# Layer 0's norms of four row tiles and layer 3's last norm: the inverse root as one power operation on GpSimd in a four-layer graph attention kernel

## The chip, the core and the metric

The kernel runs on one core of one Trainium2 chip. That core has five engines with a queue of instructions each: TensorE (PE in the profile; its weight loads are listed as PEld), VectorE (DVE), ScalarE (ACT), GpSimd (POOL) and SyncE (SP), which issues most transfers. The metric is the device time of one execution in microseconds, lower being better; of several runs the median counts. One execution of each kernel is recorded by the hardware profiler, instruction by instruction.

## The reference

Four graph attention layers over 4096 nodes of 256 features and one adjacency matrix in which a node has about 17 neighbours. Each layer ends in a residual sum and a norm, and this norm is what the change touches:

```python
def _layernorm(x, axis=-1, eps=1e-5):
    m = jnp.mean(x, axis=axis, keepdims=True)
    v = jnp.var(x, axis=axis, keepdims=True)
    return (x - m) / jnp.sqrt(v + eps)

# in a layer: projection h, then scores e[i, j] = leaky_relu(s[i] + d[j], 0.2) where adj[i, j],
# attn = softmax over j, out[i] = sum over j of attn[i, j] * h[j]   (4, 4, 2 and 1 heads)
x = _layernorm(x + layer0(x, adj))
x = _layernorm(x + layer1(x, adj))
x = _layernorm(x + layer2(x, adj))
x = _layernorm(x + layer3(x, adj))   # elu around two products; the output
```

## The kernel before

The nodes are cut into 32 row tiles of 128. A row tile does not look at all 4096 nodes: for each one the kernel packs the nodes that any of its rows has for a neighbour into 13 groups of 128, with one more place for the tile's own nodes. The packing (the class `Block`, lines 365 to 457) is done once, while layer 0 runs: VectorE compares (line 435, `oh`), TensorE moves masks with what comes out (line 441), and the lists of indices are finished ten row tiles ahead of their use.

For one row tile of one layer, `RowTile` does the following. `load` fetches the packed nodes' rows, 13 gathers by index issued on GpSimd (line 636, tile `G`), and the tile's own rows by SyncE (line 633). `half`, twice, makes the weights of 7 groups: products and exponentials on VectorE (lines 680 and 684) and ScalarE (line 689), then the mask on VectorE (lines 686 and 690, tile `w`), and TensorE sums the neighbours' rows under these weights (line 698). `finish` divides by the sum of the weights, adds the residual `y`, and calls `Layer.norm`. The normalised `y` goes to memory by SyncE (line 992), and, in layers 0 to 2, into a list `ready`, from which `Projection` takes it some steps later to make the next layer's rows (its transposition on TensorE is line 538). In layers 2 and 3 the last row tiles are also done without packing, four at a time (`whole_rows`, lines 929 to 940).

`norm` computes mean and variance of one row tile by two VectorE instructions (lines 969 and 970) into a table `mv`. It then waits until a group of row tiles has come together. `GROUPS` says how many: in layer 0 four for the row tiles 0 to 23 and one after that, so there are six groups of four; in layer 3 one for most, with row tile 27 (`count - 1`) the last to be finished and alone in its group. For the whole group at once, on tables of 128 by the size of the group, line 978 adds the small constant (tile `v`), and then the inverse root is computed without any root instruction: lines 980 and 981 make a first guess from the bits of the number, and three rounds of lines 985 to 988 improve it. These are fourteen VectorE instructions, each of which needs the one before. Line 990 then scales each row tile of the group.

The instructions of one engine run in the order in which they stand in its queue. This order is not quite that of the program: a scheduler plans all queues when the program is built, from its own estimates of durations, and puts ready work of later program lines between dependent instructions. Where two are ready, the one that stands earlier in the program comes first. The waits between engines are inserted by the same step. Tiles come from pools with fixed numbers of buffers; `G` of layer 0 has 16 slots, of which a row tile takes 7, so a gather may have to wait until TensorE is through with an older row tile.

Of the kernel before, what the change touches and what calls it, by code (L numbers as in the profile page):

```python
# [37 lines left out]
F32 = mybir.dt.float32  # L38
# [7 lines left out]
ALU = mybir.AluOpType  # L46
# [4 lines left out]
P = 128  # L51
# [4 lines left out]
BT = 4  # L56
# [79 lines left out]
@with_exitstack  # L136
def kernel(ctx: ExitStack, tc: tile.TileContext, ins: dict, out: bass.AP):
    nc = tc.nc
    const = ctx.enter_context(tc.tile_pool(name="const", bufs=1))
    dram = ctx.enter_context(tc.tile_pool(name="xs", bufs=1, space=DRAM))  # L140
    ident = const.tile([P, P], F32, name="ident")
    make_identity(nc, ident)
    shared = {
        "ident": ident,
        "idx": const.tile([P, NT, NP], I32, name="idx"),
        "flag": const.tile([1, 1], I32, name="flag"),
        "shift1": const.tile([P, 1], F32, name="shift1"),
        "shift2": const.tile([P, 1], F32, name="shift2"),
        "shift3": const.tile([4, 4], F32, name="shift3"),
        "zero": const.tile([4, 4], F32, name="zero"),  # L150
        "maskC": dram.tile([NT, P, NP, MC], U8, name="maskC"),
        "maskW": dram.tile([NB, P, NT, BT, MC], U8, name="maskW"),
        "d": [const.tile([P, NT, TERMS[n]], F32, name=f"d{n}") if WHOLE[n] else None for n in range(4)],
        "v": [dram.tile([N, ROW[n]], F32, name=f"vals{n}") for n in range(4)],
        "e": [dram.tile([NT, TERMS[n], P], F32, name=f"edge{n}") for n in range(4)],
        "x": [None] + [dram.tile([N, F], F32, name=f"xp{n}") for n in (1, 2, 3)],
    }
    nc.vector.memset(shared["shift1"], -KEXP)
    nc.vector.memset(shared["shift2"], -2.0 * KEXP)

    nc.vector.memset(shared["zero"], 0.0)
    nc.vector.memset(shared["shift3"], -2.0 * KEXP)
    nc.gpsimd.affine_select(out=shared["shift3"], in_=shared["shift3"], pattern=[[1, 4]], compare_op=ALU.is_gt,
                            fill=0.0, base=0, channel_multiplier=-1)
    with ExitStack() as packed:
        Program(tc, packed, ins, out, shared).run()
    general = nc.values_load(shared["flag"][0:1, 0:1], min_val=0, max_val=1,
                             skip_runtime_bounds_check_because="it is the result of a comparison")
    with tc.If(general > 0):
        dense_layers(tc, ins, out, ident)  # L170
# [553 lines left out]
class Layer:  # L724
# [237 lines left out]
    def norm(self, y, m):  # L962


        nc, ep = self.nc, self.prog.ep
        if not self.group:
            self.mv = ep.tile([P, BT, 2], F32, name="mv")
        st = ep.tile([P, 6], F32, name="st")
        nc.vector.bn_stats(st, y)
        nc.vector.bn_aggr(self.mv[:, len(self.group), :], st)  # L970
        self.group.append((y, m))
        if len(self.group) < next((size for end, size in GROUPS[self.n] if m < end), 1):
            return
        g = len(self.group)
        mv = self.mv[:, :g, :]

        v = ep.tile([P, BT], F32, name="v")[:, :g]
        nc.vector.tensor_scalar(v, mv[:, :, 1], EPS, None, op0=ALU.add)
        b = ep.tile([P, BT], I32, name="b")[:, :g]
        nc.vector.tensor_scalar(b, v.bitcast(I32), 1, None, op0=ALU.logical_shift_right)  # L980
        nc.vector.tensor_scalar(b, b, -1.0, float(0x5F3759DF), op0=ALU.mult, op1=ALU.add)
        r = b.bitcast(F32)
        u = ep.tile([P, BT], F32, name="u")[:, :g]
        for _ in range(3):
            nc.vector.tensor_tensor(u, r, r, op=ALU.mult)
            nc.vector.tensor_tensor(u, u, v, op=ALU.mult)
            nc.vector.tensor_scalar(u, u, -0.5, 1.5, op0=ALU.mult, op1=ALU.add)  # L987
            nc.vector.tensor_tensor(r, r, u, op=ALU.mult)  # L988
        for i, (y, m) in enumerate(self.group):
            nc.vector.tensor_scalar(y, y, mv[:, i, 0:1], r[:, i:i + 1], op0=ALU.subtract, op1=ALU.mult)  # L990
            dst = self.prog.out if self.n == 3 else self.shared["x"][self.n + 1]
            nc.sync.dma_start(out=dst[m * P:(m + 1) * P, :], in_=y)
            if self.n < 3:
                self.ready.append((self.step + 1, y, m))
        self.group = []
# [39 lines left out]
def dense_layers(ctx: ExitStack, tc: tile.TileContext, ins: dict, out: bass.AP, ident):  # L1035
# [361 lines left out]
    def layer(nodes, following):  # L1397
        n = nodes.n
        nxt = following() if following is not None else None
        for blk in range(NB):  # L1400
# [13 lines left out]
            else:  # L1414
# [6 lines left out]
                for it in range(BT):  # L1421
# [8 lines left out]
                    nc.vector.scalar_tensor_tensor(yt, z, 0.0, yt, op0=ALU.max, op1=ALU.add)  # L1430
                    nc.vector.scalar_tensor_tensor(yt, e, -1.0, yt, op0=ALU.add, op1=ALU.add)
            norm(y)
            dst = out if n == 3 else xD[n + 1]
            nc.sync.dma_start(out=to_tiles(dst[blk * W:(blk + 1) * W, :]), in_=y)
# [57 lines left out]
```

## Time and profile before

| | us |
|---|---|
| median of 3 runs | 2267.64 (2262.25 to 2268.71) |
| the profiled execution | 2271.01 |
| its span, first to last recorded instruction | 2269.3 |
| busy: PE, DVE, ACT, POOL | 2019.7, 1798.0, 1738.5, 1494.7 |

The span counts from the first instruction to the last; the execution's own time has 1.7 us more around it. The page of the profile cuts the span into 40 slices and gives each engine's busy share in each, in tenths. Other views give busy times by stretch, groups of instructions by line, who waited for whom, and the instructions in order of time; in the last of these, a line has the start in us from the start of the span, the duration, the engine, the line of the program, the operation, the tiles that it writes and reads, their shapes, and in brackets how long the engine was idle before it and what ended that. TensorE's busy time includes modelled ends, so a high number does not mean that it runs at its peak. From the first use of gathered rows to the last of layer 0 is about 165 to 820 us, layer 1 runs to some 1340, layer 2 to some 1750, and layer 3 to the end. The groups of instructions that belong to the fourteen are these:

```profile
L987 DVE TENSOR_SCALAR u<-u 128x1 f32<-128x1 f32 (+2 forms) x237 | 38.6, 165 | 3.6
L988 DVE TENSOR_TENSOR b<-b,u 128x1 f32<-128x1 f32 (+2 forms) x237 | 37.1, 158 | 3.7
L985 DVE TENSOR_TENSOR u<-b 128x1 f32<-128x1 f32 (+2 forms) x237 | 37.0, 158 | 3.2
L986 DVE TENSOR_TENSOR u<-u,v 128x1 f32<-128x1 f32 (+2 forms) x237 | 37.0, 158 | 3.4
L980 DVE TENSOR_SCALAR b<-v 128x1 int32<-128x1 int32 (+2 forms) x79 | 13.3, 169 | 1.0
L981 DVE TENSOR_SCALAR b<-b 128x1 int32<-128x1 int32 (+2 forms) x79 | 13.2, 169 | 1.0
```

After the count stand the group's busy time in us, the mean duration of one in ns, and the engine's idle time before them in us.

### The profile page before, as it was taken

To read this page: it belongs to the slowest core of one execution; us is meant where nothing else is said; L and a number is where in the kernel's file an instruction comes from. 1 tells how busy PE (TensorE), PEld (TensorE's weight loads), DVE (VectorE), ACT (ScalarE), POOL (GpSimd) and SP (SyncE) were. 2 spreads that over 40 slices of the span, in tenths; PEclk is the share of its full clock that TensorE was granted. 3 is DMA by queue.
4 is the path that set the end of the run, shared out by engine and by line. 5 is a ranking of instruction groups with operands and counts; after the bars stand their busy time and mean duration, and the time that the engine had idled before them with its cause. 6 is when DMAs were issued, how large, how long until landed. Compare 5 with 4: busy or idle time off the path is not lost. (4 is left out here: it accounts for less than half of the span.)

```text
span 2269.3 us, 49072 instructions
## 1 busy us (share of the span) xinstructions
PE 2019.7 (89%) x15689; PEld 1834.6 (81%) x15689; DVE 1798.0 (79%) x5317; ACT 1738.5 (77%) x4977; POOL 1494.7 (66%) x1596
## 2 busy tenths in 40 slices
PE   3878889989999959998988897989998799999996
PEld 2757878887989949998878887989997688778885
DVE  2987999999999959988888886877975465576567
ACT  4777888988889949988888877978883666676664
POOL 2107565655667777777777777777761677777773
PEclk8988999999999979999999998999998899999998
DMA  8879767877557766666666666778764788888884
GB/s 281 264 229 356 237 213 248 292 240 233 143 163 194 211 165 167 190 177 174 166 173 176 172 169 180 216 206 239 221 200 138 236 268 269 274 266 276 266 256 145
DMA packets 250318, 492.98 MB, mean 217 GB/s; under 512 B 44385, under 2 KB 156610, under 8 KB 249666
## 3 DMA queue, kind: packets, MB, share of 16 engines
q0 software_dynamic: 81536, 245.30, 38.0%
q1 hardware_dynamic: 168514, 244.46, 33.7%
q8 instruction: 126, 2.06, 0.4%
q14 instruction: 142, 1.16, 0.2%
HBM read 437.05 MB, written 52.54 MB: 216 GB/s over the span
## 5 line engine op out<-in xcount | busy, mean ns | idle before, releaser
L636 POOL DMA_INDIRECT G<-vals,idx x1456 | 1481.7, 1018 | 736.4 <-issue 188.5
L689 ACT ACTIVATE w<-S,G 128x128 f32<-128x128 f32 x3248 | 988.2, 389 | 123.0 <-DMA G<-vals,idx 109.1
L698 PE MATMUL bank<-w,G 128*65 128x128 f32 x7168 | 843.8, 277 | 97.8 <-DVE w L686 75.7
L698 PEld LDWEIGHTS bank<-w,G 128*65 128x65 f32 x7168 | 796.4, 140 | 116.5 <-DVE w L686 86.9
L701 PE MATMUL bank<-G,w 128*128 128x257 f32 (+1 forms) x2688 | 491.1, 340 | 36.1 <-DVE w L690 12.5
L701 PEld LDWEIGHTS bank<-G,w 128*128 128x128 f32 x2688 | 431.8, 193 | 86.2 <-ACT z L1004 16.6
L690 DVE SCALAR_TENSOR_TENSOR w<-w,bank 128x896 f32<-128x896 f32 x384 | 410.6, 1079 | 18.7 <-ACT w L689 18.1
L940 PE MATMUL bank<-vw,pw 128*128 128x129 f32 (+1 forms) x2048 | 299.7, 303 | 5.6 <-ACT zw L1004 2.7
L940 PEld LDWEIGHTS bank<-vw,pw 128*128 128x128 f32 x2048 | 275.7, 193 | 22.4 <-ACT zw L1004 3.1
L666 ACT ACTIVATE w<-S,G 128x128 f32<-128x128 f32 x392 | 138.0, 390 | 130.0 <-DMA G<-vals 77.6
L435 DVE TENSOR_SCALAR oh<-iota,place 128x256 bf16<-128x256 f16 (+2 forms) x992 | 225.8, 301 | 9.3 <-PE bank L441 9.3
L441 PE MATMUL bank<-mk,oh 128*128 128x132 fp8e4 x2336 | 188.6, 226 | 12.4 <-DVE oh L435 10.2
L680 DVE TENSOR_TENSOR w<-S,G 128x256 f32<-128x256 f32 x384 | 154.0, 417 | 53.0 <-DMA G<-vals,idx 49.6
L552 PE MATMUL bank<-wext,xT 128*128 128x268 f32 (+3 forms) x640 | 181.4, 417 | 15.7 <-ACT xT L543 12.8
L441 PEld LDWEIGHTS <-oh 128*128 128x128 bf16 x2336 | 148.6, 99 | 48.3 <-DVE oh L435 20.4
L380 ACT ACTIVATE mk<-raw 128x1024 uint8<-128x1024 int32 x128 | 131.1, 1054 | 25.8 <-DMA raw<-in_adjB_dram 25.1
L552 PEld LDWEIGHTS bank<-wext,xT 128*128 128x128 f32 x640 | 119.2, 203 | 35.5 <-ACT xT L543 15.7
L929 ACT ACTIVATE pw<-Sw,d 128x512 f32<-128x512 f32 x192 | 131.7, 714 | 15.6 <-PE bank L940 11.9
L937 DVE TENSOR_TENSOR pw<-pw,mw 128x512 f32<-128x512 f32 x64 | 44.1, 693 | 125.0 <-ACT pw L936 61.6
L930 DVE SCALAR_TENSOR_TENSOR pw<-pw,mw 128x512 f32<-128x512 f32 x192 | 126.7, 690 | 17.3 <-ACT pw L929 16.4
L686 DVE SCALAR_TENSOR_TENSOR w<-w,bank 128x896 f32<-128x896 f32 x128 | 138.6, 1083 | 0.8
L690 DVE SCALAR_TENSOR_TENSOR w<-w,mk 128x896 f32<-128x896 f32 x80 | 86.7, 1087 | 47.5 <-ACT w L689 44.1
(131 smaller groups left out, 1605.3 us busy)
## 6 DMA issues: line engine op xcount, KB each, us to landing
raw<-in_adjB_dram SPq DMA_DIRECT2D x128, 512.0 KB
mk<-maskC SPq DMA_DIRECT2D x112, 231.0 KB
G<-vals,idx POOLq DMA_INDIRECT x1456
S<-edge SPq DMA_DIRECT2D x64, 256.0 KB
vw<-vals SPq DMA_DIRECT2D x96, 129.0 KB
xp<-y SPq DMA_DIRECT2D x96, 128.0 KB
y<-xp SPq DMA_DIRECT2D x96, 128.0 KB
mw<-maskW SPq DMA_DIRECT2D x20, 528.0 KB
```

Of the source, the lines that this page charges most:

```text
L435: nc.vector.tensor_scalar(oh[:, :n * P], iota[:, :n * P], self.place[:, it, j:j + 1], None, op0=ALU.is_equal)
L441: nc.tensor.matmul(accs[b][:, s * MC:(s + 1) * MC], oh[:, (k - a) * P:(k - a + 1) * P], mk[:, j, it, :].bitcast(FP8), start=touches[b][0] ...
L552: nc.tensor.matmul(pp[:, :c1 - c0], self.xT[:, k, :], wext[:, k, c0:c1], start=(k == 0), stop=(k == KT - 1 and brow is None))
L636: nc.gpsimd.indirect_dma_start(out=self.place(pos), out_offset=None, in_=sh["v"][n][:NODES[t], :], in_offset=bass.IndirectOffsetOnAxis(ap= ...
L666: nc.scalar.activation(w[0][:, k, :], S[:, 0, :], AF.Relu, bias=d(k, 0))
L680: nc.vector.tensor_tensor(w[h][:, k:k + 2, :], S[:, h:h + 1, :].to_broadcast([P, 2, P]), dd[:, :, V + T + h:V + T + h + 1].to_broadcast([P ...
L686: nc.vector.scalar_tensor_tensor(w[h], w[h], LEAST, mh, op0=ALU.max, op1=ALU.mult)
L689: nc.scalar.activation(w[h][:, k, :], S[:, h, :], AF.Exp, bias=d(k, h))
L690: nc.vector.scalar_tensor_tensor(w[h], w[h], LEAST, mh, op0=ALU.max, op1=ALU.mult)
L698: nc.tensor.matmul(accs[0][:Wd, h * P:(h + 1) * P], v, w[h][:, k, :], **how)
L701: nc.tensor.matmul(a, w[h][:, k, :], v, **how)
L940: nc.tensor.matmul(accs[it][:, c:c + Wd], p[:, it, :], v[:, c:c + Wd], start=(j == 0 and h == heads[0]), stop=(j == NT - 1), skip_group_ch ...
```

## The change

For the six groups of four in layer 0 and for the last norm of layer 3, `norm` leaves the fourteen instructions out. In their place GpSimd raises `v` to the power −0.5, elementwise, in one instruction on 128 by 4 (or 128 by 1) numbers, with the exponent from a table `mhalf` that is filled once at the start. The scaling is moved into a function of its own that both ways call. All other norms are as before.

```diff
@@ -143,6 +143,7 @@
         "idx": const.tile([P, NT, NP], I32, name="idx"),
+        "mhalf": const.tile([P, BT], F32, name="mhalf"),
         "flag": const.tile([1, 1], I32, name="flag"),
@@ -155,6 +156,7 @@
+    nc.vector.memset(shared["mhalf"], -0.5)
     nc.vector.memset(shared["shift1"], -KEXP)
@@ -976,6 +978,12 @@
         nc.vector.tensor_scalar(v, mv[:, :, 1], EPS, None, op0=ALU.add)
+        if self.n == 0 and g == BT or self.n == 3 and m == self.count - 1:
+
+            r = ep.tile([P, BT], F32, name="r")[:, :g]
+            nc.gpsimd.tensor_tensor(r, v, self.shared["mhalf"][:, :g], op=ALU.pow)
+            self.scale(mv, r)
+            return
         b = ep.tile([P, BT], I32, name="b")[:, :g]
@@ -986,6 +994,10 @@
             nc.vector.tensor_tensor(r, r, u, op=ALU.mult)
+        self.scale(mv, r)
+
+    def scale(self, mv, r):
+        nc = self.nc
         for i, (y, m) in enumerate(self.group):
             nc.vector.tensor_scalar(y, y, mv[:, i, 0:1], r[:, i:i + 1], op0=ALU.subtract, op1=ALU.mult)
             dst = self.prog.out if self.n == 3 else self.shared["x"][self.n + 1]
```

## The prediction

> **What bounds the kernel now.** I read the page first, for the busy tenths of each engine, then the same by stretches of layer 0, then who waits there, then the instructions around one norm, and last the end of the program. The page shows a kernel whose bound changes:
>
> ```profile
> span 2269.3 us, 49072 instructions
> PE   3878889989999959998988897989998799999996
> DVE  2987999999999959988888886877975465576567
> POOL 2107565655667777777777777777761677777773
> ```
>
> Each digit is 57 us. From the fifth slice to the fourteenth (227 to 794 us, nearly all of layer 0) VectorE stands at 9; in the last third it falls to 4 to 7, with TensorE at 9. So the same instruction saved on VectorE is worth something in layer 0 and next to nothing later. The stretches from one norm of four to the next make it sharp (columns: length, then busy us and count of PE, PEld, DVE, ACT and POOL, the granted clock, DMA share, GB/s):
>
> ```profile
> 284.00:372.00 88.00, 78.66 (x789) 70.29 (x786) 87.60 (x273) 78.72 (x232) 52.86 (x54) 1.00 0.74 234
> 547.00:632.00 85.00, 79.91 (x789) 73.77 (x789) 84.52 (x273) 62.95 (x212) 52.72 (x53) 0.96 0.57 171
> 632.00:697.00 65.00, 62.39 (x572) 59.20 (x573) 62.53 (x157) 57.90 (x202) 45.18 (x47) 1.00 0.62 171
> 697.00:822.00 125.00, 118.72 (x1036) 113.63 (x1033) 116.89 (x357) 108.44 (x375) 95.14 (x99) 1.00 0.71 199
> ```
>
> Up to 632 us VectorE is idle 0.4 to 0.5 us in 87, and TensorE 5 to 9. The waits of TensorE from 160 to 822 us agree: 30.5 us of them end with the weights of line 686 and 9.3 us with those of line 690, both VectorE's. GpSimd has 32 us or more of each free. After 632 us, when the packing of the lists runs out, TensorE and VectorE stand within 2 us of each other.
>
> How often the changed code runs is in the answer for the line of v:
>
> ```profile
> L978 DVE TENSOR_SCALAR v<-mv x79: 140/155/310, 283.6 to 2260.1; 128x1 f32<-128x1 f32 x43, 128x2 f32<-128x2 f32 x29, 128x4 f32<-128x4 f32 x6, 128x3 f32<-128x3 f32 x1
> ```
>
> There are 79 norms; the six of width 4 are layer 0's row tiles 0 to 23, with v at 283.6, 371.1, 458.2, 546.7, 631.0 and 695.1 us. Here is VectorE in time (start, duration) around the first, then GpSimd at the same moment:
>
> ```profile
> 283.62 0.19 DVE L978 TENSOR_SCALAR v<-mv 128x4 f32<-128x4 f32 x1
> 283.72 0.27 DVE L684 TENSOR_SCALAR w<-S,G 128x128 f32<-128x128 f32 x1
> 283.92 0.16 DVE L980 TENSOR_SCALAR b<-v 128x4 int32<-128x4 int32 x1
> 283.99 0.24 DVE L435 TENSOR_SCALAR oh<-iota,place 128x128 bf16<-128x128 f16 x1
> ...
> 284.22 1.07 DVE L686 SCALAR_TENSOR_TENSOR w<-w,bank 128x896 f32<-128x896 f32 x1
> 285.22 0.15 DVE L985 TENSOR_TENSOR u<-b 128x4 f32<-128x4 f32 x1
> 285.29 1.07 DVE L690 SCALAR_TENSOR_TENSOR w<-w,bank 128x896 f32<-128x896 f32 x1
> ...
> 292.23 1.05 DVE L990 TENSOR_SCALAR y<-y,mv,b 128x256 f32<-128x256 f32 x3
> ```
>
> ```profile
> 278.18 0.95 POOL L636 DMA_INDIRECT G<-vals,idx  x1 [0.30 <-issue]
> 283.42 1.14 POOL L636 DMA_INDIRECT G<-vals,idx  x1 [4.30 <-DVE mv L970]
> 284.87 0.95 POOL L636 DMA_INDIRECT G<-vals,idx  x1 [0.31 <-DVE b L981]
> ```
>
> Two things are to be seen. The fourteen small instructions of the root are not run one after another: other work stands between them, so the order was planned, and v to y takes 8.6 us without VectorE resting. And GpSimd's gathers come in a dense row, 1.25 us from start to start, that begins just before v. Last, the end of the program, where nothing else is left:
>
> ```profile
> 2260.12 0.15 DVE L978 TENSOR_SCALAR v<-mv 128x1 f32<-128x1 f32 x1
> 2260.31 0.15 DVE L980 TENSOR_SCALAR b<-v 128x1 int32<-128x1 int32 x1
> ...
> 2262.80 0.16 DVE L988 TENSOR_TENSOR b<-b,u 128x1 f32<-128x1 f32 x1
> 2263.00 0.41 DVE L990 TENSOR_SCALAR y<-y,mv,b 128x256 f32<-128x256 f32 x1
> 2263.44 0.33 SPq L992 DMA_DIRECT2D out_dram<-y  x1
> ```
>
> **What the Trainium skill says.** "VectorE: DVE Perf Modes", section "The DRAIN you can't avoid", has it that VectorE's instructions are to be counted, not their semaphores, since the next one waits for the pipe to empty. The trace agrees in part: alone a small one costs 0.19 us (the tail), between others far less (below). "GPSIMD Engine Reference", section 3.1, gives 4497 ns for an add of 2048 elements per partition at about 2.6 cycles an element; at the page's 1.2 GHz that leaves some 60 ns of fixed cost. No page prices a power, and the trace of before has none. "Perfetto Trace Analysis", section "GPSIMD Engine Instruction", advises to take GpSimd by start-to-start spacing: here a gather shows 0.95 us and recurs every 1.25. "SBUF — State Buffer", section "Who interferes with whom", says that a GpSimd read of SBUF and a VectorE instruction with two SBUF inputs exclude each other; line 680 is one, of 0.4 us. The kernel before has no GpSimd elementwise work in layer 0, so its trace can't show this.
>
> **The change, part by part.** *Layer 0, VectorE.* Each norm of four loses 14 instructions: lines 980 and 981, and three rounds of four. In the first, the time from the start of each of the fourteen to the start of the next instruction is 0.07 us ten or eleven times, else 0.08 to 0.12, together 1.1 us. The other way: v to y holds 17 other instructions, which at their usual spacing (1.00 us for lines 686 and 690, for instance) fill 7.3 of the 8.6 us; the rest is 1.3 us. The second way gives 1.1 to 1.3 us for the five norms up to 631 us. I take 1.15: five of them, 5.8 us, on an engine with no idle time, so on the path. The sixth lies where VectorE and TensorE are level: I take half, 0.5 us. That is 6.3 us, as long as TensorE, idle 5 to 9 us a stretch there, doesn't take over at 1.15.
>
> *Layer 0, GpSimd.* One power is added per norm, with two waits: it for v, and the first scaling (line 990) for it. Crossing from VectorE to GpSimd took 0.07 us at the start of the program (the table bt: 13.54 to 13.61); I take the same back. The power on 128x4: below, the smallest dependent GpSimd operations there (0.28 us); above, 2 us, an estimate of mine at seven times that, for a function made of many steps. I take 0.8. Before it there may be a gather in progress, up to 1.25 us, and a read held off by line 680, up to 0.4. So the root lands 0.9 to 3.8 us after v, most likely about 1.5, where it took 7.3 to 8.3 until now. Behind the power stand the gathers of two tiles further on; a delay of 1 us is nothing to them (VectorE's waits for gathers in 160 to 822 us are 3.2 us in all). Behind the waiting scaling stands everything of VectorE: the masked weights that TensorE waits for. This costs nothing if the plan puts lines 684, 435 and 686 in between, as now (1.4 us at their spacing), and the lateness in full if not. I take nothing, and 0 to 2.5 us each as the bounds.
>
> *The last norm of layer 3.* From line 980 to the scaling there are 2.69 us with nothing beside. In their place: 0.07 + 0.8 + 0.07, with the usual 0.04 us of crossing already in the old spacing: some 0.9. The gain is 1.8 us on the path (bounds 2.3 and 0.5), as the output's transfer starts after it. The norm before it, in 2253.7 to 2256.4, keeps its fourteen.
>
> *The fill of the table of −0.5, the tile r, the moved scaling loop:* one VectorE instruction of some 0.06 us at the start, when the engine is idle for 10 us; nothing.
>
> Sum: 5.8 + 0.5 + 1.8 = 8.1 us. The profiled execution of before took 2271.01 us (span 2269.3), so 2262.9 of its kind; the median of the runs is 3.4 us lower, 2267.64, which gives 2259.5.
>
> **The rivals.** *A, the forecast (0.54):* as summed, own range 2255 to 2263.
>
> *B, the saving is given back (0.21):* waits of about 0.7 us for the root at each of six norms take 4 us, or TensorE and its clock (0.96 in 459 to 632 us) become the bound of these stretches. For it: TensorE is at 91 to 94% there. Against: it waits for VectorE, not the other way round. About 2264.
>
> *C, the root lands too late and VectorE stands (0.17):* the power takes 2 us or more, or is queued behind two gathers, and the scaling is put where a short power would be ready. Landing 4.5 us after v with 1.4 us of cover is a stop of 3.1 us, six times 18.6; less the 6.3 saved and with 0.5 left of the tail, 11.8 slower: 2279. It decides from a stop of 1.2 us per norm on, where 6.3 + 0.5 to 1.8 are eaten. For it: gathers are dense just after v, VectorE runs in order, and no row prices a power. Against: GpSimd is 38% free or more up to 632 us, and the power is older in the program than the gathers of tile m+3 that run there.
>
> *D, the new order helps more than its saving (0.08):* y comes 5 us earlier, and the whole plan shifts with it; TensorE's waits for line 686 in 160 to 822 us (30.5 us) shrink by a quarter: 2252.
>
> **How the numbers follow.** A measurement of this kernel tells some 0.3% from no change (6.8 us; the three runs lie within 6.5). Seven tenths of A lie below 2260.8 (0.38); with D and a tenth of B that is 0.48 for faster. The rest of A and of B, 0.16 and 0.19, is no change, 0.35. C is slower, 0.17. Range 2252 to 2274: it takes in A, B and the milder half of C.
>
> **What would show it.** 72 chains of line 988 in place of 79 (216 instructions for 237); seven powers on GpSimd, each of 0.3 to 1 us; v to y in the six norms at 1.5 to 3 us; no VectorE idle time put down to GpSimd; VectorE still without idle time to 620 us, and the sixth norm 5 to 6 us sooner; tail from v to scaling about 1.1 us instead of 2.9. Wrong it would be if the waits view has VectorE's line 990 behind GpSimd for over 1 us a time, if the sixth norm comes no sooner, or if layers 1 to 3 change length by more than 3 us, which this sum doesn't have.

## The result and the profile after

The changed kernel takes 2296.86 us (median of 4 runs, 2295.89 to 2297.24), the kernel before 2264.94 us on the same chip (4 runs, 2259.79 to 2268.71). The ratio is 1.0133, with a 95% interval of 1.0113 to 1.0154: 1.3% slower, where 8 us less were forecast. The page of the changed kernel has these lines against those of before:

```profile
span 2295.2 us, 48988 instructions
PE   4888898988988987998989898989998799999996
DVE  2887998989988977998888895878885366566566
POOL 2117655646567777777777777777871677777773
```

VectorE has 97 instructions fewer (seven times fourteen, less one fill) and is no longer solid 9 from the fifth slice on: it has less work and stands still more. The stretches from norm to norm of layer 0 say how much longer it takes (columns as before: length, busy us and count of PE, PEld, DVE, ACT, POOL, granted clock, DMA share, GB/s):

```profile
282.00:372.00 90.00, 81.88 (x791) 73.73 (x789) 86.56 (x262) 76.77 (x225) 54.36 (x55) 0.96 0.72 231
561.40:652.00 90.60, 79.72 (x786) 73.14 (x786) 82.98 (x258) 61.27 (x207) 51.52 (x54) 0.96 0.52 161
652.00:722.00 70.00, 64.68 (x574) 61.76 (x573) 62.31 (x144) 58.45 (x205) 47.07 (x48) 0.95 0.56 158
722.00:848.00 126.00, 117.28 (x1024) 114.28 (x1022) 115.11 (x339) 107.31 (x374) 96.03 (x100) 0.96 0.67 192
```

The third stretch is 70 us instead of 64, the second 90.6 instead of 84.3. From the first norm of layer 0 to its last (`v` to `v`) the changed kernel takes 561.8 us and the one before 532.3, so 29.5 us more; from there to the end of the program they take 1451.4 and 1453.4. So the loss is all in layer 0. VectorE's waits between these norms (for whom, total us, times, longest), after and then before:

```profile
DVE y L1002 <- POOL r L984: 27.3, 6, 9.6
DVE oh L437 <- PE bank L443: 9.9, 5, 2.4
DVE w L692 <- ACT w L691: 5.0, 7, 2.5
```

```profile
DVE w L690 <- ACT w L689: 1.7, 6, 0.7
DVE oh L435 <- PE bank L441: 0.2, 1, 0.2
```

There are six waits of 27.3 us in all for the power's result `r`, which the kernel before does not have, and 9.9 us for TensorE's mask products, which were 0.2 us before. Here is the second of the six in time, first VectorE, then GpSimd:

```profile
371.95 0.18 DVE L980 TENSOR_SCALAR v<-mv 128x4 f32<-128x4 f32 x1
372.04 0.24 DVE L437 TENSOR_SCALAR oh<-iota,place 128x128 bf16<-128x128 f16 x1
372.20 1.07 DVE L688 SCALAR_TENSOR_TENSOR w<-w,bank 128x896 f32<-128x896 f32 x1
377.78 1.40 DVE L1002 TENSOR_SCALAR y<-y,mv,r 128x256 f32<-128x256 f32 x4 [4.50 <-POOL r L984]
```

```profile
370.50 1.10 POOL L638 DMA_INDIRECT G<-vals,idx  x1 [3.20 <-PE bank L700]
371.91 0.98 POOL L638 DMA_INDIRECT G<-vals,idx  x1 [0.30 <-DVE mv L972]
373.20 0.96 POOL L638 DMA_INDIRECT G<-vals,idx  x1 [0.30 <-issue]
374.46 0.96 POOL L638 DMA_INDIRECT G<-vals,idx  x1 [0.30 <-issue]
375.72 0.96 POOL L638 DMA_INDIRECT G<-vals,idx  x1 [0.30 <-issue]
376.70 1.04 POOL L984 TENSOR_TENSOR r<-v,mhalf 128x4 f32<-128x4 f32 x1
```

`v` is ready at 372.13. VectorE has 1.1 us of other work left in front of the scaling and then stands for 4.5 us with its whole queue behind it. GpSimd does not take long over the power: it issues four gathers first, one every 1.26 to 1.29 us, and only then comes to the power, which takes 1.04 us. At the six norms the power starts 2.0, 4.6, 3.6, 5.0, 3.1 and 9.6 us after the end of `v` (2, 4, 3, 4, 3 and 8 gathers in front, with the one in progress), and the idle times before the scaling are 1.8, 4.5, 3.5, 4.9, 3.0 and 9.6 us.

The stops did not all cost the same. From the first of the six norms to the sixth the changed kernel takes 440.1 us for 411.5, so 28.6 us more, with 17.7 us of stops in them. From the sixth norm to the last of layer 0 it takes 121.7 us for 120.8, though the longest stop, 9.6 us, lies there. In that stretch it is GpSimd that does not rest. In the kernel before, its last longer pause in layer 0 ends at 652.74 us, and from there to the last norm 128 gathers follow each other with never more than 0.31 us between them. The place where this begins (before), and the sixth norm's power in this row (after):

```profile
645.70 0.95 POOL L636 DMA_INDIRECT G<-vals,idx  x1 [0.31 <-issue]
652.74 1.12 POOL L636 DMA_INDIRECT G<-vals,idx  x1 [6.10 <-ACT w L689]
654.17 0.95 POOL L636 DMA_INDIRECT G<-vals,idx  x1 [0.30 <-issue]
```

```profile
730.87 0.96 POOL L638 DMA_INDIRECT G<-vals,idx  x1 [0.30 <-issue]
731.85 1.04 POOL L984 TENSOR_TENSOR r<-v,mhalf 128x4 f32<-128x4 f32 x1
733.07 1.01 POOL L638 DMA_INDIRECT G<-vals,idx  x1 [0.18 <-issue]
```

The stop of VectorE does not interrupt the row: from the sixth norm to the last of layer 0 GpSimd issues 95 gathers in both kernels. So the traces speak for the row of gathers as what sets the pace there, rather than VectorE; no run tests this by itself.

At the end of the program GpSimd's queue is empty, and the forecast holds:

```profile
2284.43 0.15 DVE L980 TENSOR_SCALAR v<-mv 128x1 f32<-128x1 f32 x1
2284.74 0.57 POOL L984 TENSOR_TENSOR r<-v,mhalf 128x1 f32<-128x1 f32 x1 [18.36 <-DVE v L980]
2285.35 0.41 DVE L1002 TENSOR_SCALAR y<-y,mv,r 128x256 f32<-128x256 f32 x1 [0.76 <-POOL r L984]
```

From `v` to the scaling are 0.92 us, where it was 2.88.

### The profile page after: what moved, and what is told of

Its sections match the earlier page's. It is cut to its first block, busy times and chain, and to the rows that moved or that the text cites. A ratio compares the mean times of both kernels' runs of the same rounds, so it can differ in the third digit from the quotient of the medians.

```text
span 2295.2 us, 48988 instructions
## 1 busy us (share of the span) xinstructions
PE 2032.6 (89%) x15689; PEld 1844.6 (80%) x15689; DVE 1790.5 (78%) x5220; ACT 1739.6 (76%) x4977; POOL 1503.9 (66%) x1603
## 5 line engine op out<-in xcount | busy, mean ns | idle before, releaser
L700 PE MATMUL bank<-w,G 128*65 128x128 f32 x7168 | 853.1, 279 | 114.8 <-DVE w L688 64.8
L700 PEld LDWEIGHTS bank<-w,G 128*65 128x65 f32 x7168 | 805.3, 141 | 135.2 <-DVE w L688 74.7
L692 DVE SCALAR_TENSOR_TENSOR w<-w,bank 128x896 f32<-128x896 f32 x384 | 409.9, 1078 | 22.4 <-ACT w L691 21.5
L450 ACT ACTIVATE cm<-bank 128x396 uint8<-128x396 f32 (+1 forms) x160 | 68.7, 451 | 87.5 <-PE bank L443 86.7
```

The lines of the kernel that those rows point to most:

```text
L692: nc.vector.scalar_tensor_tensor(w[h], w[h], LEAST, mh, op0=ALU.max, op1=ALU.mult)
L700: nc.tensor.matmul(accs[0][:Wd, h * P:(h + 1) * P], v, w[h][:, k, :], **how)
```

## The experiments

Eighteen runs were made beside the kernel before, in five sets. They came to chips of two kinds, and the numbers cannot be read without this: on some the kernel before takes about 2267 us, on others 2764 to 2799 us. On the latter TensorE stands still without a releaser that the profile shows, and the clock that it was granted was 0.88 to 0.90 of full speed over a whole run, against 0.95 to 0.97 on the others; why is not known. Waits of TensorE in the whole of the kernel "late" on such a chip, and VectorE's longest in 338 to 905 us, its layer 0:

```profile
PE bank L700 <- issue: 168.1, 222, 2.5
PE bank L703 <- issue: 81.2, 73, 8.3
```

```profile
DVE oh L437 <- PE bank L443: 81.6, 72, 6.7
```

There VectorE itself has long waits for TensorE in layer 0 (81.6 us at that line, 0.2 us in the kernel before above), so these chips say little about a stop of VectorE on a chip like that of the result. The times are medians. Ratios are to the kernel before on the same chip; they come from all runs and can differ a little from the quotient of the medians. The last column is VectorE's wait for the root in the recorded execution.

| kernel | before, us | this, us | ratio (95%) | wait, us |
|---|---|---|---|---|
| the change | 2264.94 | 2296.86 | 1.0133 (1.0113 to 1.0154) | 28.1 |
| change_again | 2267.59 | 2296.80 | 1.0130 (1.0100 to 1.0161) | 29.6 |
| trip_again | 2267.59 | 2298.10 | 1.0134 (1.0104 to 1.0163) | 30.7 |
| ahead_again | 2267.59 | 2275.20 | 1.0036 (1.0023 to 1.0048) | 6.5 |
| both | 2267.59 | 2267.28 | 1.0008 (0.9994 to 1.0023) | 5.7 |
| both26 | 2268.71 | 2273.72 | 1.0020 (1.0011 to 1.0029) | 1.0 |
| both26_raw5 | 2268.71 | 2270.97 | 1.0009 (0.9996 to 1.0021) | 1.0 |
| before_raw5 | 2268.71 | 2267.84 | 0.9995 (0.9986 to 1.0004) | none |
| tail_again | 2268.71 | 2269.51 | 1.0004 (0.9992 to 1.0017) | 0.7 |
| tail | 2799.22 | 2805.04 | 1.0015 (0.9995 to 1.0036) | 0.7 |
| ahead | 2799.22 | 2803.69 | 1.0013 (0.9993 to 1.0033) | 1.8 |
| late | 2799.22 | 2792.67 | 0.9976 (0.9960 to 0.9993) | 10.3 |
| trip | 2799.22 | 2803.37 | 1.0015 (0.9999 to 1.0031) | 33.5 |
| first3 | 2766.46 | 2770.58 | 1.0018 (1.0005 to 1.0031) | 11.9 |
| five_raw5 | 2766.46 | 2764.93 | 0.9993 (0.9969 to 1.0016) | 0.8 |

The remaining four runs, all on the second kind of chip, are told below.

**The change again (change_again).** The same kernel, beside the others of its set:

> The changed kernel once more, beside the kernel before on whatever chip this is. Where the kernel before takes about 2265 us, VectorE bounds layer 0 and it should be 30 us slower, with 27 us of VectorE's waits for the root there. Where the kernel before takes about 2800 us, as in the first four experiments, TensorE stands still for 30 us of 120 without a visible reason, VectorE has idle time to give, and theory of the queue expects the same waits of 20 us or more but less than 10 us in the time. The rival, that the new order as such costs the 30 us, expects them on both.

It was 29 us slower, with the same waits at the same places. The other half of the question, the change on a chip of the second kind, was not run.

**The last norm alone (tail, tail_again).** The condition is cut to layer 3:

```diff
-        if self.n == 0 and g == BT or self.n == 3 and m == self.count - 1:
+        if self.n == 3 and m == self.count - 1:
```

> Only the last norm of layer 3 takes the power; layer 0 is as before. The trace of the change shows v to scaling there in 0.92 us where 2.88 stood, so both theories expect the time of before less 2 us, about 2263 against 2265, and layers 0 to 2 of unchanged length within 3 us. If the new order of the whole program were what costs 30 us, some of it would be seen here already: more than 5 us slower than before would speak for that.

> The power in the last norm alone, where the kernel before takes 2265: v to scaling in 0.92 us for 2.88, so 2 us less, within what can be told from no change; layer 0 as before within 3 us.

Both are no change that can be told, and in both traces `v` to the scaling takes under 1 us. In "tail_again" layer 0 keeps its length: 533.8 us from first to last norm, against 532.3 before. The 2 us are gained in the trace and are too few for the medians to show. A price of 30 us that comes with the changed program as such is excluded by "tail_again"; what a new order within layer 0 costs, this run does not say.

**The wait alone (trip, trip_again).** The fourteen instructions stay; a copy through GpSimd is put behind them in the same seven norms:

```diff
+        if self.n == 0 and g == BT or self.n == 3 and m == self.count - 1:
+            far = ep.tile([P, BT], F32, name="far")[:, :g]
+            nc.gpsimd.tensor_copy(far, r)
+            r = far
         self.scale(mv, r)
```

> The fourteen instructions are kept and a copy of the root through GpSimd is added, in the same seven norms: the wait alone, with nothing saved and no power. Theory of the queue: the copy meets the row of gathers later, 7 us after v, when it is still dense, so VectorE waits 1 to 4 us at each, 6 to 25 us in all, and the time is before plus that, 2271 to 2292. Rival (the power is slow): a copy of 0.3 us leaves waits under 0.7 us each, and the time is that of before within 5 us.

> The fourteen instructions kept, with the copy through GpSimd, which showed 33 us of waits of VectorE in the six norms of layer 0 in the first experiments. Where the kernel before takes 2265 us: the queue alone expects 25 to 45 us more, 2290 to 2310, more than the change itself, as nothing is saved; the rival of a slow power, or of a new order around a shorter chain, expects under 10 us. Where it takes 2800 us: within 8 us of before.

This is the clearest answer. The copy takes 0.20 us and there is no power in the program, yet the kernel is as slow as the change, 1.0134, and VectorE's waits, this time for the copy `far`, are of the same kind:

```profile
DVE y L1000 <- POOL far L993: 30.3, 6, 11.9
DVE rec L1026 <- PE bank L718: 3.4, 3, 1.7
```

There are 30.3 us of waits in layer 0 and 30.5 us more in the median: on this kind of chip the stops of VectorE in layer 0 cost, taken together, what they last. The sixth of them, 11.9 us, does interrupt GpSimd's row of gathers (for 5.7 us), and from the sixth norm to the last of layer 0 this kernel takes 129.7 us for 120.8. On the other kind ("trip") 33.2 us of idle time before the six scalings went with 4 us more, which is not clear of no change.

**The power ahead of the gathers (ahead, ahead_again).** The gathers of places 10 to 13 of the row tile three further on are queued behind the power of that norm:

```diff
-            nc.gpsimd.tensor_tensor(r, v, self.shared["mhalf"][:, :g], op=ALU.pow)
+            power = nc.gpsimd.tensor_tensor(r, v, self.shared["mhalf"][:, :g], op=ALU.pow)
+            if self.n == 0:
+                self.prog.power[m + 3] = power.ins
...
+            with ExitStack() as order:
+                if n == 0 and pos >= 10 and m in prog.power:
+                    order.enter_context(prog.tc.issue_after(prog.power[m]))
                 nc.gpsimd.indirect_dma_start(
```

> All seven powers stay; the gathers of places 10 to 13 of the row tile three further on are queued behind the power, which so stands ahead of them in GpSimd's queue. Theory of the queue (the power waits behind 2 to 8 gathers of 1.25 us, and VectorE's whole queue behind it): the power starts within 0.1 us of v, the root lands 1.3 us after v, VectorE's waits for GpSimd fall from 28 us to under 4, and the time is before less 3 to 8 us, 2257 to 2262. Rival (the power itself, or the crossing between engines, is slow): waits of 2 us or more each stay, and the time stays over 2285. Second rival (the new order of the other instructions): the waits go, but 9 us or more of the 32 stay.

> The power ahead of the gathers, as in the second experiment. Where the kernel before takes 2265 us: theory of the queue expects 2257 to 2263, since the fourteen instructions are gone and VectorE waits under 4 us for the root; the rival of the new order expects 2270 or more. Where it takes 2800 us: within 8 us of before.

The second norm of "ahead_again", GpSimd and then VectorE:

```profile
366.37 0.95 POOL L642 DMA_INDIRECT G<-vals,idx  x1 [0.31 <-issue]
372.04 1.04 POOL L988 TENSOR_TENSOR r<-v,mhalf 128x4 f32<-128x4 f32 x1 [4.72 <-DVE v L984]
373.28 1.14 POOL L642 DMA_INDIRECT G<-vals,idx  x1 [0.19 <-ACT w L695]
```

```profile
371.80 0.16 DVE L984 TENSOR_SCALAR v<-mv 128x4 f32<-128x4 f32 x1
372.03 1.08 DVE L692 SCALAR_TENSOR_TENSOR w<-w,bank 128x896 f32<-128x896 f32 x1
373.12 1.40 DVE L1008 TENSOR_SCALAR y<-y,mv,r 128x256 f32<-128x256 f32 x4
```

The power now starts 0.08 us after `v`, its 1.04 us lie beside line 692, and no wait is left at this norm. The ratio falls from 1.0130 to 1.0036: of 29 us of loss by medians, 22 go with the place of the power in GpSimd's queue. The first rival (a slow power or crossing) falls. But the kernel was expected at 2257 to 2263 us, faster than before, and takes 2275, where the rival of the new order was put. Of waits for the root 4.9 us remain at the sixth norm, where gathers of lower places still come first, and 0.8 at the first; VectorE's waits for ScalarE at line 696 are 7.4 us, for 1.7 at that instruction before. So the rival, that other waits take over, is alive.

**The scaling later (late, both).** The scalings of layer 0's fours are kept back half a row tile in the program: alone ("late"), and with the power ahead ("both"):

```diff
-            self.scale(mv, r)
+            if self.n == 0:
+                self.owed = (mv, r, self.group)
+                self.group = []
+            else:
+                self.scale(mv, r)
             return
...
             self.tile(m).half(part)
+        if self.owed is not None:
+            mv, r, self.group = self.owed
+            self.owed = None
+            self.scale(mv, r)
```

> All seven powers stay where they are in GpSimd's queue, and the four scalings of layer 0's groups are written half a row tile later in the program, which puts 2 to 3 more instructions of 1 us ahead of them in VectorE's queue. Theory of the queue: the power still lands 2 to 6 us after v, but 2 to 3 us more of it are covered; VectorE's waits for GpSimd fall from 28 us to 10 to 16, and the time to 2275 to 2285. Rival (new order, not the waits): no change from 2297.

> The power ahead of the gathers, and the scalings of layer 0 half a row tile later in the program: no wait for the root is left in layer 0 at all. Theory of the queue: VectorE's waits for GpSimd under 1.5 us, all in the last norm, and the time of the kernel with the power ahead less 0 to 3 us: 2255 to 2262 where before takes 2265. Rival of the new order: 2270 or more.

"late" came to a chip of the second kind: the waits fell to 10.3 us, as expected, and it was 0.24% faster there than the kernel before, the only one of all with an interval below 1; the clock granted was 0.891 in the mean of its runs and 0.889 in those of the kernel before, so this is no clean sign of the order alone. What it does on the other kind of chip was not run. "both" has no wait at the first five norms and is level with the kernel before, 1.0008: the loss is gone, but 2255 to 2262 us were expected, and the 6 us of VectorE's time and the 2 us of the tail that it saves do not show. From the first norm to the sixth it takes 413.5 us (411.5 before), from there to the last of layer 0, where the gathers run without a pause, 122.1 (120.8). Its own waits in layer 0 (282 to 819 us) tell where the time went, with ScalarE and VectorE in order of time behind them:

```profile
DVE w L696 <- ACT w L695: 7.3, 9, 2.9
DVE y L1017 <- POOL r L993: 4.9, 1, 4.9
DVE row L581 <- ACT row L579: 2.5, 2, 2.2
```

```profile
394.59 1.06 ACT L383 ACTIVATE mk<-raw 128x1024 uint8<-128x1024 int32 x1 [3.07 <-DMA raw<-in_adjB_dram]
395.55 2.72 ACT L695 ACTIVATE w<-S,G 128x128 f32<-128x128 f32 x9
```

```profile
397.72 1.09 DVE L696 SCALAR_TENSOR_TENSOR w<-w,bank 128x896 f32<-128x896 f32 x1 [2.67 <-ACT w L695]
```

In this order ScalarE converts the next adjacency rows at 387 us, where it did so at 400 us before; the fifth of them has not landed yet, ScalarE stands 3.1 us, and VectorE 2.7 us behind it. This wait did not exist in this part of the kernel before.

**The sixth norm's gathers and the rows' buffer (both26, both26_raw5, before_raw5).** "both26" is "both" with the gathers of row tile 26 held back from place 4 on; "both26_raw5" has five buffers for the adjacency rows in addition; "before_raw5" is the kernel before with the five buffers alone:

```diff
-                if n == 0 and pos >= 10 and m in prog.power:
+                if n == 0 and pos >= (4 if m == 26 else 10) and m in prog.power:
...
-        cst, rawp, mkp, ohp = pool("icst", 1), pool("raw", 4), pool("imk", 2), pool("oh", 8)
+        cst, rawp, mkp, ohp = pool("icst", 1), pool("raw", 5), pool("imk", 2), pool("oh", 8)
```

> As the kernel with the power ahead and the later scaling, but the gathers of row tile 26 are held back from place 4 on, since there the sixth power still met a gather row (a wait of 4.9 us). Theory of the queue: VectorE's waits for GpSimd under 1.5 us in all; the time 4 to 5 us below that kernel's: where before takes 2267, 2261 to 2264. If the time stays at 2267, what is left comes from elsewhere: a rival says that the granted clock or TensorE bounds layer 0 once the waits are gone.

> The same with a fifth buffer for the adjacency rows. In the kernel with the power ahead and the later scaling, ScalarE waited twice 3 us for such rows in layer 0 and VectorE behind it 5.8 us, which the kernel before does not show there. If that is where the rest of the saving went, these waits go and the time is another 3 to 6 us lower, 2256 to 2260 where before takes 2267; if TensorE bounds the stage, nothing changes.

> The kernel before with the fifth buffer alone. It has no such waits in 283 to 640 us, so the theory expects no change (within 3 us). If it is as much faster as the kernel above, the buffer has nothing to do with the root.

The sixth wait went (0.2 us left in layer 0), and the time rose all the same, to 1.0020, where 2261 to 2264 us had been expected. From the sixth norm to the last of layer 0 it takes 128.2 us where "both" took 122.1. GpSimd stands 1.6 us before the power there, and the gathers held back, with all those queued after them, come later; in the last 72 us (751 to 823) ScalarE waits for gathers (8.9 us; 6.1 at the end of layer 0 before) and VectorE 6.3 us for ScalarE:

```profile
ACT w L695 <- DMA G<-vals,idx: 8.9, 5, 3.6
ACT row L573 <- PE bank L555: 4.1, 1, 4.1
```

The fifth buffer takes ScalarE's waits for adjacency rows from 6.3 to 1.6 us and the five stretches from the first norm to the sixth from 414.9 to 410.3 us (411.5 before). The whole is 1.0009, level with the kernel before, where 2256 to 2260 us had been expected: the 4.6 us are seen in the trace, and in the medians 2.75 us. The buffer alone makes no difference to the kernel before that can be told, 0.9995. So behind each wait that was taken away stood another, within a few us.

**Some of the norms (first3, sixth, five, five_raw5, first3_again, five_raw5_again).** The condition is cut to row tiles below 12, to the group of 20 to 23, or to the first five groups with the two edits of "both", without and with the fifth buffer:

```diff
-        if self.n == 0 and g == BT or self.n == 3 and m == self.count - 1:
+        if self.n == 0 and g == BT and m < 12:
```

> The power as in the change, in the groups of row tiles 0 to 11 alone, three of the six; the rest and the last norm as before. Theory of the queue: the price goes with the waits of these three, 10 to 12 us in the change's traces, less 3 x 1.15 saved, with the time that TensorE and VectorE lose to each other behind a stop on top (9 us for six): 9 to 14 us slower than before. Rival of the new order (a fixed price of a rebuilt plan): either about nothing or nearly the whole 30.

> The power as in the change, in the group of row tiles 20 to 23 alone. In the change's traces the stop there was 9.65 us, behind eight gathers; here the power stands three gathers nearer, so 5 to 6 us. Theory of the queue: 3 to 8 us slower than before, as TensorE and VectorE are level there. Rival: no change, as it is one norm.

> The power ahead of the gathers and the later scaling, in the first five groups and the last norm; the sixth keeps its fourteen instructions, and no gathers of row tile 26 are held back. No wait for the root is left in layer 0, nor the 9 us that the last stretch of layer 0 lost to late gathers when those were held. Theory: 2262 to 2267 where before takes 2268; what is missing from 8 us goes to the waits for adjacency rows.

> The same with the fifth buffer for adjacency rows, which took 4.6 us off the five stretches between the norms when both other parts were in. Theory: 3 to 5 us below the kernel without it, 2259 to 2263 where before takes 2268, the first that is faster than before beyond its interval. If TensorE has become the bound of layer 0, it stays at 2265 or more.

> The power as in the change in the first three groups alone, once more, on a chip where the kernel before takes about 2267 us if it comes to that. Theory of the queue: the waits of these three are 10 to 12 us, less 3.4 saved, with what TensorE and VectorE lose to each other behind a stop on top: 9 to 14 us slower. Rival of a fixed price for a rebuilt plan: nothing, or nearly 30.

> The power ahead of the gathers and the later scaling in the first five groups, a fifth buffer for adjacency rows, the sixth group with its fourteen instructions, the power in the last norm; on a chip where the kernel before takes about 2267 us if it comes to that. Theory: 2258 to 2263, faster than before beyond its interval. If TensorE has become the bound of layer 0, 2265 or more.

All came to chips of the second kind, the repeats of "first3" and "five_raw5" too. "first3" has its waits (11.9 us) and takes 1.0018 of the time before (1.0005 to 1.0031), the repeat 1.0008 (0.9993 to 1.0024); "sixth" 0.9982 (0.9959 to 1.0004), where the power happened to meet no gather; "five" 1.0015 (0.9995 to 1.0035); "five_raw5" 0.9993 and its repeat 0.9995 (0.9981 to 1.0009). They don't decide what they were for: whether the price adds up over the norms when the power is taken in some of them only, and whether the last version would beat the kernel before on a chip like that of the result. Both are open.

## Why the prediction was wrong, point by point

- *What bounds layer 0.* Right up to the sixth norm: VectorE has 4.3 us of idle time in 411.5 there, and with "trip_again" it is shown that stops of it in layer 0 cost, taken together, what they last. Behind the sixth norm the forecast set VectorE and TensorE level and left out GpSimd, whose gathers follow each other without a pause from 653 us on. A saving on VectorE could hardly show there, and the stop of 9.6 us hardly did.
- *The saving on VectorE.* Right in kind and near in size: from first to last norm it is busy 517.7 us instead of 523.3, so 5.6 us less against 6.9 counted for six norms (6.3 put on the path).
- *The tail.* Right: 1.96 us gained for 1.8 forecast.
- *The power's own time.* It took 1.04 to 1.07 us on 128 by 4, where 0.8 was assumed, well within the bounds; it is not the cause. The 0.4 us that the forecast allowed for a read held off by VectorE do not show in these times.
- *"The root lands 0.9 to 3.8 us after v, most likely about 1.5", and "This costs nothing if the plan puts lines 684, 435 and 686 in between, as now".* This is the step that failed. The root landed 3.1 to 10.6 us after `v`. One gather in progress was allowed for; two to eight stood in front. The reason given against it, that the power "is older in the program than the gathers of tile m+3", did not hold in the queue as built: the power does come first in the program, and the plan put those gathers before it all the same. The other reason, that GpSimd "is 38% free or more", counts the 0.3 us between two gathers as free, which are half of the 32 us in 547 to 632 us, and says nothing of the moment of `v`. The cover, VectorE's other work between `v` and the scaling, was 1.0 to 1.3 us for 1.4 forecast, so all the rest was a stop: 27.3 us in six. The trace of before had the sign: a row of gathers every 1.25 us that starts with `v`, in a queue that runs in order. And the sign that the forecast named for being wrong, line 990 behind GpSimd for over 1 us a time, came at all six norms.
- *Rival C* named this mechanism and its place, with a chance of 0.17. It was priced at two gathers and 3.1 us a stop, 11.8 us in all; it came to 4.6 us a stop.
- *The sum after the waits.* 27.3 us of stops less 5.6 saved are 22, and layer 0 lost 29.5. The rest is VectorE's waits for TensorE (line 437, +9.7 us) and for ScalarE (line 692, +3.3 us), less some 5 us of other waits that the kernel before had and this one has not. All of the waits at line 437 lie before the sixth norm. TensorE was busy 504 us for 497 in this part, at a granted clock of 0.96 for 0.98. "trip_again", with stops as long, has the same 504 us and 0.96, but no such waits for TensorE, so where they come from is open. The lower clock goes with the stops: over whole runs it was 0.956 in the mean for "change_again" and "trip_again", and 0.960 to 0.962 for the kernel before, "ahead_again" and "both" beside them. Which of the two brings the other was not tried.
- *The forecast's other half,* that without stops 8 us would be won, was not met either. "both" has 4.9 us of stops left and by the forecast's 8.1 us should have been about 3 us faster; it was level. Up to the sixth norm the saved time went into waits for ScalarE, and through it for adjacency rows, that the order of before did not have (the fifth buffer brought 4.6 us of it back); behind it the pace is the gathers'. Rival B (the saving is given back) was right in what came of it, but by neither of its reasons, waits of 0.7 us for the root or TensorE as the bound.

## What to carry to other kernels

Before a dependent step is moved to another engine, look at that engine's queue at the very moment when the operand is ready: what is queued there, and is it in order? A free share of 38% over a stretch says little if the free time lies elsewhere in it; what has to be compared is the arrival in the queue with the work that the asking engine still has in hand. And where one engine is only a little busier than the others, its saved time soon goes into the next wait: here the six chains of fourteen small instructions could be taken out without the kernel getting faster.

## What the runs showed of the hardware that had not been expected

- A power on GpSimd took 1.04 us on 128 by 4 numbers and 0.57 us on 128 by 1, some 0.16 us for each further number per partition by this difference; a copy of 128 by 4 took 0.20 us. The Trainium skill's "GPSIMD Engine Reference", section 3.1, has some 2.6 cycles an element for an add; at the page's 1.2 GHz that is, as an estimate, 0.002 us. The page gives no rate for a power, and that of an add does not serve for it: the measurement decides.
- A power that follows a gather started within 0.03 us of its end and the next gather 0.18 to 0.19 us after the power, where gathers in a row have 0.3 us between them.
- Crossing from VectorE to GpSimd took 0.09 to 0.15 us when the queue was empty, and back 0.04 us or less.
- Two kinds of chip differed by 22 to 23% in the time of the same kernel, with VectorE's and ScalarE's instructions as long on both (1080 and 389 ns for lines 692 and 691 in "late", 1078 and 389 in the change). The copy through GpSimd that cost 1.3% on one ("trip_again") went with 0.15% on the other ("trip"), which is not clear of no change.
